# A graph-attention kernel: scores and exponential of a unit set a round ahead of its weights and sums

## The chip, the cores and the metric

The kernel runs on one core of a Trainium2 chip. A core has five engines with an instruction stream each: TensorE (PE, with its weight loads shown as PEld), VectorE (DVE), ScalarE (ACT), GpSimd (POOL) and SyncE (SP); sixteen DMA engines move data for the queues of SP, ACT and POOL. Each engine takes its instructions in order and waits on semaphores of the others. The metric is the device time of one execution in microseconds (us), lower is better; the time stated is the median of three runs.

## The reference

Three layers of graph attention with one head over N = 6250 nodes of D = 64 features and 206250 edges that come ordered by target node (`dst`); between the layers a normalisation, and at the end the logarithm of a softmax, the residual and a last normalisation:

```
def _transformer_conv(x, src, dst, edge_attr, Wq, bq, Wk, bk, Wv, bv, We, Ws, bs):
    q = x @ Wq + bq
    k = x @ Wk + bk
    v = x @ Wv + bv
    e = edge_attr @ We
    kj = k[src] + e
    alpha = jnp.sum(q[dst] * kj, axis=-1) / jnp.sqrt(jnp.float32(D))
    amax = jax.ops.segment_max(alpha, dst, num_segments=N)
    p = jnp.exp(alpha - amax[dst])
    denom = jax.ops.segment_sum(p, dst, num_segments=N)
    w = p / denom[dst]
    msg = (v[src] + e) * w[:, None]
    agg = jax.ops.segment_sum(msg, dst, num_segments=N)
    return agg + x @ Ws + bs

for i in range(L):
    x = _transformer_conv(x, src, dst, edge_attr, Wq[i], ...)
    x = jax.nn.relu(x)
    if i < L - 1:
        x = _layer_norm(x, ln_gamma[i], ln_beta[i])
return jax.nn.log_softmax(x, axis=1)
```

## The kernel before

The edges are cut into chunks of 512, four chunks (`LB`) to a *unit*. A loop goes over the units of a layer, one unit a *round*; the order of instructions on every engine is the order in which the program writes them (a manual schedule), so the calls in the loop of `main_path` are the order of the work.

For one unit, with features of the source nodes beside edge features in a buffer `feat` (edges on partitions):

- `turn(0)` and `turn(1)`: TensorE transposes two chunks each into a PSUM tile of tag "a" (L1517), ScalarE copies them into `featT` (L1520); the edge half of `featT` comes by a load of SP from `eaS` (`across`, L1496).
- `scores`: four matmuls mark in which of a chunk's 32 node slots each edge lies (L1528), four more multiply the queries `q` with `featT` (L1530), into the PSUM tile `ps_s`. The four chunks use the four groups of 32 columns of the array. VectorE takes the maximum `most` (L1537) and its negative (L1539), ScalarE the exponential `prob` (L1541). `prob` has one buffer.
- `weights`: TensorE transposes `prob` (L1549); the copy `probT` (L1552) is ScalarE's in layer 0 and VectorE's in layers 1 and 2. `probT` has one buffer.
- `sums`: sixteen matmuls of `probT` with `feat` (L1562), copied by ScalarE to `part` (L1570). A later `store` writes it to tables in DRAM (L1576). After its sums a unit's `feat` is free: `room` starts the load of the edge half of a later unit into that buffer (`fetch`, SP, L558). There are four buffers (`FB`).

In round u the turns are those of unit u, while scores, weights and sums are those of unit u-1, in this order: turn 0, scores, a bank of picks, turn 1, weights, naturals, a second bank, sums. So weights wait in the same round for the scores' maximum and exponential.

Beside this run, in every round:

- Gathers. GpSimd fetches rows of source nodes by indirect DMA (L609), each released by a small ScalarE copy, the *gate* (L608), which `drip` and `free` place between other work. Layer 0 gathers twelve times a unit, two units ahead.
- Picks and naturals. For part of the edges the source rows come from SBUF: VectorE writes one-hot masks `hot` (six for a bank, L1208, `aim`), TensorE multiplies them with the node table (twelve matmuls, L1234, `bank`), ScalarE copies the result to `kept` (L1241). In odd rounds `naturals` turns `kept` into features of the next pair of units (L1251), which VectorE copies into `feat` (L1268, L1270).
- In layer 0 alone: sorting. `move` advances a generator that sorts the edge features of a later unit with bf16 matmuls against masks `hit` that VectorE makes (`hit` L992, products L1004, stamps L1013, twice a round one half), drains them by ScalarE (`to` L1024, `eT` L1027 and their DMA issues L1028 and L1031), transposes and writes them (L1037, L1039, L1042), and computes indices (L1050, L1052, `src_b` L1053).

Between layers the last three units run in a tail, node features are finished and written (`finish`), and the first loads of the next layer start. PSUM has a tile ring for each tag ("a", "g", "m", "p", "s", "x").

Of the kernel before, what the change touches and what calls it, by code (L numbers as in the profile page):

```python
# [9 lines left out]
F32 = mybir.dt.float32  # L10
# [9 lines left out]
P = 128  # L20
D = 64
L = 3
# [406 lines left out]
def main_path(  # L429
# [123 lines left out]
    def fetch(layer, k):  # L553

        c0, m = batches[k]
        feat = feats.tile([P, LB * T * 2 * D], F32, name="feat")
        if placed(layer, k):
            nc.sync.dma_start(feat[:, LB * T * D :], eaP[k])  # L558
        if layer or placed(layer, k):
            feat = feat.rearrange("p (h c t d) -> p c t h d", h=2, c=LB, d=D)  # L560
        else:
            feat = feat.rearrange("p (c t h d) -> p c t h d", h=2, c=LB, d=D)
        if not placed(layer, k):
            nc.sync.dma_start(
                feat[:, :m, :, 1].rearrange("p c t d -> p (c t) d"),
                ea[c0 : c0 + m].rearrange("c (t p) d -> p (c t) d", p=P),
            )
        loaded[layer, k] = feat
# [604 lines left out]
    class Picker:  # L1173
# [25 lines left out]
        def aim(self):  # L1199

            self.load()
            if not self.aims or self.aims[0][:2] not in self.keys or self.hots:
                return
            k, t, i = self.aims.pop(0)
            made = []
            for h in range(BW):
                hot = picks.tile([P, 2 * PAIR * W], F32R, name="hot", bufs=BW)
                nc.vector.tensor_scalar(  # L1208
                    hot,
                    self.keys[k, t][:, 2 * i * PAIR * W : 2 * (i + 1) * PAIR * W],  # L1210
                    rank[:, h : h + 1],
                    None,
                    ALU.is_equal,
                )
                made.append(hot)
            self.hots[k, t, i] = made
            if i == QUARTERS // 2 - 1:
                del self.keys[k, t]
            self.load()

        def bank(self, tag="x"):

            if not self.banks:
                return
            self.aim()
            k, t, i = self.banks.pop(0)
            made = self.hots.pop((k, t, i))
            px = ps(tag)
            for q in range(2):
                for h in range(BW):  # L1230
                    b = (t * QUARTERS + 2 * i + q) * BW + h
                    assert halved[b] == self.layer
                    cols = slice(q * PAIR * W, (q + 1) * PAIR * W)
                    nc.tensor.matmul(  # L1234
                        px[:, cols],
                        halves[b >= EARLY][:, b - EARLY * (b >= EARLY)].rearrange("p h d -> p (h d)"),
                        made[h][:, cols],
                        start=(h == 0),
                        stop=(h == BW - 1),
                    )  # L1240
            nc.scalar.copy(  # L1241
                kept[t][:, :, 2 * i : 2 * i + 2].rearrange("p c q e -> p q c e"),
                px.rearrange("p (q c e) -> p q c e", q=2, e=W),
            )
            if self.layer:
                self.aim()

        def natural(self, k, t, c, out):

# [199 lines left out]
    class Unit:  # L1449
# [73 lines left out]
        def scores(self, bank):  # L1523
            n = self.rows
            self.p_s = ps(bank)
            quarters = [slice(slot(j) * W, (slot(j) + 1) * W) for j in range(n // W)]
            for j, rows in enumerate(quarters):
                nc.tensor.matmul(self.p_s[rows], codeT[:, rows], self.to, start=True, stop=(j >= self.m))  # L1528
            for j, rows in enumerate(quarters[: self.m]):
                nc.tensor.matmul(  # L1530
                    self.p_s[rows], self.q[:, j * STRIDE : j * STRIDE + W], self.featT[:, j, :], start=False, stop=True
                )
# [4 lines left out]
            nc.vector.tensor_reduce(top[:n], self.p_s[:n], AX.X, ALU.max)  # L1537
            neg = self.part[:n, P : P + 1]
            nc.vector.tensor_scalar(neg, top[:n], -1.0, -M_INIT, ALU.mult, ALU.min)  # L1539
            self.prob = work.tile([P, CH], F32, name="prob", bufs=1)  # L1540
            nc.scalar.activation(  # L1541
                self.prob[:n], self.p_s[:n], AF.Exp, bias=neg, accum_out=self.part[:n, P + 1 : P + 2]
            )

        def weights(self):
# [70 lines left out]
    def serve():  # L1616

        while rooms:
            layer, k = rooms[0]
            if k < len(batches):  # L1620
# [1 line left out]
                    return  # L1622
                fetch(layer, k)
                await_turn(layer, k)
            elif layer + 1 < L and k - len(batches) < FB:
                if not layer and k - len(batches) not in moved:
                    return
                fetch(layer + 1, k - len(batches))
# [13 lines left out]
    class Line:  # L1642
# [7 lines left out]
        def sums(self, to):  # L1650
            for u in range(self.summed, to):
                chunks[self.layer, u].sums()
                if units[u][1] == LB or u == NU - 1:
                    room(self.layer, u + FB if units[u][1] == LB else len(batches) - 1 + FB)
                self.summed = u + 1

        def weights(self, to):
# [1 line left out]
                chunks[self.layer, u].weights()  # L1659
                self.weighed = u + 1  # L1660

        def scores(self, to, bank="s"):
            for u in range(self.scored, to):
                chunks[self.layer, u].scores(bank)
                self.scored = u + 1

        def store(self):
# [19 lines left out]
    for layer in range(L):  # L1687
# [13 lines left out]
        for u in range(NU - 3):  # L1701
# [4 lines left out]
            line.store()  # L1706
            if waiting:
                active.append(waiting.pop(0))
            close_up()
            points = [0]  # L1710
            this.turn(0, lambda: drip(u))
            close_up(3) if close else step()
            move(paces[0])
            if not layer:
                drip(u, 2)
            move(paces[1])
            line.scores(u)
# [21 lines left out]
            move(paces[3])  # L1739
            if not layer:  # L1740
                drip(u, 2)
            line.sums(u)
            free(u, LB - 1)
            picker.aim()

        more = layer + 1 < L
        for _ in sorting:
# [126 lines left out]
```

## Time and profile before

| | us |
|---|---|
| median of three runs | 5328.32 |
| lowest and highest of them | 5322.16, 5331.89 |
| the profiled execution | 5337.1 |
| its span on the core | 5335.4 |
| first round of layer 0 to its last | 119 to 2453 |
| the same in layer 1 | 2524 to 3881 |
| the same in layer 2 | 3955 to 5291 |

The mean granted clock of TensorE in the profiled execution was 0.857 of full speed. The profile's groups give for a line, engine and operation the number of instructions, their busy time and mean length, and then the idle time of that engine just before them with what ended most of it ("<-ACT prob L1541": the engine was idle until ScalarE's instruction of line 1541 that writes `prob`). "issue" stands for idle time in which the engine waited for nothing that the profile shows; "remote" for a semaphore event whose origin is not among the core's recorded instructions. Ends of matmuls are modelled. An fp32 matmul shows as two records. The recorded chain of waits is empty for this execution, so the argument goes by groups, stretches and timelines.

### The profile page before, as it was taken

To read this page: it belongs to the slowest core of one execution; us is meant where nothing else is said; L and a number is where in the kernel's file an instruction comes from. 1 tells how busy PE (TensorE), PEld (TensorE's weight loads), DVE (VectorE), ACT (ScalarE), POOL (GpSimd) and SP (SyncE) were. 2 spreads that over 40 slices of the span, in tenths; PEclk is the share of its full clock that TensorE was granted. 3 is DMA by queue.
4 is the path that set the end of the run, shared out by engine and by line. 5 is a ranking of instruction groups with operands and counts; after the bars stand their busy time and mean duration, and the time that the engine had idled before them with its cause. 6 is when DMAs were issued, how large, how long until landed. Compare 5 with 4: busy or idle time off the path is not lost.

```text
span 5335.4 us, 105267 instructions
## 1 busy us (share of the span) xinstructions
PE 4095.7 (77%) x33967; PEld 2681.4 (50%) x33967; DVE 3172.4 (59%) x8763; ACT 2099.4 (39%) x6475; POOL 2914.4 (55%) x2863
## 2 busy tenths in 40 slices
PE   5677777777777777776788888888768878887876
PEld 3344444444444444444565555555545555555553
DVE  5556666566666656554566656666445666666664
ACT  1233344334434334333344444444333444444443
POOL 4445555555555545553666566665536666666663
PEclk9788999889999988887888888888878888888887
DMA  6555665566666556553555555555435555555553
GB/s 138 138 142 138 157 159 149 151 156 157 156 155 160 149 154 159 141 154 99 126 138 137 127 135 138 140 137 128 120 89 134 135 131 136 137 139 135 135 136 85
DMA packets 749708, 737.55 MB, mean 138 GB/s; under 512 B 390960, under 2 KB 501578, under 8 KB 749150
## 3 DMA queue, kind: packets, MB, share of 16 engines
q1 hardware_dynamic: 565854, 510.70, 38.3%
q0 software_dynamic: 91264, 93.64, 10.3%
q10 hardware_dynamic: 92032, 126.38, 7.1%
q8 instruction: 276, 4.52, 0.4%
q14 instruction: 282, 2.31, 0.1%
HBM read 570.27 MB, written 160.07 MB: 137 GB/s over the span
## 4 chain that ended last, share of the span: by engine, by line


## 5 line engine op out<-in xcount | busy, mean ns | idle before, releaser
L609 POOL DMA_INDIRECT feat<-x,gate x1608 | 1661.9, 1033 | 1055.6 <-ACT gate L608 556.5
L609 POOL DMA_INDIRECT feat<-in_x,gate x1212 | 1218.1, 1005 | 1199.3 <-ACT gate L608 534.3
L1208 DVE TENSOR_SCALAR hot<-key,rank 128x512 fp32r<-128x512 f16 x2976 | 1254.1, 487 | 284.6 <-remote 104.7
L1234 PE MATMUL ps_x<-hot,halves 128*128 128x256 f32 x4800 | 845.3, 322 | 35.9 <-issue 17.8
L1234 PEld LDWEIGHTS ps_x<-hot,halves 128*128 128x128 f32 x4800 | 704.3, 214 | 321.8 <-issue 178.1
L1520 ACT COPY featT<-ps_a 64x512 f32<-64x512 f32 x1192 | 690.4, 579 | 172.5 <-issue 47.3
L1537 DVE TENSOR_REDUCE most<-ps_s 128x1 f32<-128x512 f32 x297 | 205.0, 690 | 813.1 <-PE ps_s L1530 447.6
L1562 PE MATMUL ps_g<-feat,probT 128*32 128x128 f32 x9672 | 512.3, 309 | 212.6 <-issue 161.1
L1530 PE MATMUL ps_s<-featT,q 128*32 128x512 f32 x2376 | 517.3, 727 | 57.6 <-issue 49.5
L608 ACT COPY gate<-src_b 128x1 int32<-128x1 int32 x2772 | 501.8, 191 | 122.4 <-issue 52.2
L1241 ACT CAST kept<-ps_x 128x512 fp32r<-128x512 f32 x400 | 234.8, 587 | 792.1 <-remote 511.9
L1004 PE MATMUL ps_x<-hit,rest 128*64 128x512 bf16 x3200 | 534.2, 414 | 4.0 <-issue 3.7
L1562 PEld LDWEIGHTS ps_g<-feat,probT 128*32 128x32 f32 x9672 | 337.2, 122 | 360.4 <-issue 253.1
L1541 ACT ACTIVATE prob<-ps_s,part 128x512 f32<-128x512 f32 x297 | 204.4, 688 | 760.6 <-DVE part L1539 520.2
L1549 PE MATMUL ps_p<-ident,prob 128*128 128x128 f32 (+1 forms) x1224 | 218.8, 306 | 347.1 <-ACT prob L1541 283.3
L992 DVE TENSOR_SCALAR hit<-ruler,pos 128x512 bf16<-128x512 f16 x1600 | 483.1, 373 | 2.7 <-remote 2.7
L1517 PE MATMUL ps_a<-ident,feat 128*128 128x128 f32 x2380 | 438.1, 307 | 45.0 <-issue 30.9
L1517 PEld LDWEIGHTS ps_a<-ident,feat 128*128 128x128 f32 x2380 | 303.8, 157 | 171.3 <-issue 128.2
L1004 PE MATMUL ps_x<-hit,raw 128*64 128x512 bf16 x1600 | 347.4, 427 | 8.6 <-issue 8.6
L1549 PEld LDWEIGHTS ps_p<-ident,prob 128*128 128x128 f32 (+1 forms) x1224 | 144.3, 152 | 402.5 <-ACT prob L1541 322.6
L1004 PEld LDWEIGHTS <-rest 128*64 128x64 bf16 x3200 | 201.2, 121 | 181.2 <-issue 59.0
L1570 ACT COPY part<-ps_g 128x128 f32<-128x128 f32 (+1 forms) x309 | 81.4, 263 | 408.2 <-remote 115.0
(235 smaller groups left out, 4618.5 us busy)
## 6 DMA issues: line engine op xcount, KB each, us to landing
feat<-eaP SPq DMA_DIRECT2D x296, 512.0 KB
featT<-eaS SPq DMA_DIRECT2D x296, 512.0 KB
key<-keyS SPq DMA_DIRECT2D x248, 256.0 KB
raw<-in_ea SPq DMA_DIRECT2D x200, 256.0 KB
eaS<-eT ACTq DMA_DIRECT2D x200, 256.0 KB
eaP<-eN ACTq DMA_DIRECT2D x200, 256.0 KB
feat<-x,gate POOLq DMA_INDIRECT x1608
part<-part SPq DMA_DIRECT2D x600, 32.5 KB
```

What stands on the lines that cost most here:

```text
L608: copy(gate, index[:, i + t : i + t + 1])
L609: nc.gpsimd.indirect_dma_start(out=loaded[layer, k][:, c, t, 0], out_offset=None, in_=xts[layer][:, :], in_offset=bass.IndirectOffsetOnAxi ...
L992: nc.vector.tensor_scalar(hit, ruler, self.pos[:, at : at + 1], None, ALU.is_equal)
L1004: nc.tensor.matmul(self.px[i][j * D : (j + 1) * D, :], self.part(i, part)[:, (j * T + t) * D : (j * T + t + 1) * D], self.hits[t, 2 * i + ...
L1208: nc.vector.tensor_scalar(hot, self.keys[k, t][:, 2 * i * PAIR * W : 2 * (i + 1) * PAIR * W], rank[:, h : h + 1], None, ALU.is_equal,)
L1234: nc.tensor.matmul(px[:, cols], halves[b >= EARLY][:, b - EARLY * (b >= EARLY)].rearrange("p h d -> p (h d)"), made[h][:, cols], start=(h ...
L1241: nc.scalar.copy(kept[t][:, :, 2 * i : 2 * i + 2].rearrange("p c q e -> p q c e"), px.rearrange("p (q c e) -> p q c e", q=2, e=W),)
L1517: nc.tensor.transpose(pt[:, j - js[0], t // 2], rows[:, t * D : (t + 2) * D], ident)
L1520: nc.scalar.copy(featT[:, :, :, h, :], pt[h * D : (h + 1) * D])
L1530: nc.tensor.matmul(self.p_s[rows], self.q[:, j * STRIDE : j * STRIDE + W], self.featT[:, j, :], start=False, stop=True)
L1549: nc.tensor.transpose(p_t[:, t, :n], self.prob[:n, t * P : (t + 1) * P], ident[:n, :n])
L1562: nc.tensor.matmul(p_g[rows, :].rearrange("n (h d) -> n h d", h=2), self.probT[:, t, rows], batch[:, c + j, t], start=(t == 0), stop=(t == ...
```

## The change

In round u the weights (transposes and copy) and the sums are now those of unit u-2, while the scores remain those of unit u-1. Weights open the round, the sums stand before the scores, and the exponential is a method of its own, `exps`, called after turn 1. The new order in a round: weights (u-2), turn 0, in layers 1 and 2 a bank, sums (u-2), scores (u-1), in layer 0's odd rounds a bank, turn 1, exponential (u-1), naturals, a bank.

With it: naturals and the second bank use the PSUM tag "p" in place of "s"; in layers 1 and 2 the masks of a bank may be made two banks ahead, with a second set of six `hot` buffers in the pool `later`; a fifth feature buffer in layers 1 and 2, also in `later` (every fifth batch uses it), so that `room` and `serve` count five there; the gates of layer 0 stand at other places of the round (`drip`); at a layer switch one more batch is fetched. In the tail weights precede sums. Lines from about 557 on move by 3 to 10.

```
-        feat = feats.tile([P, LB * T * 2 * D], F32, name="feat")
+        more = layer and ((layer - 1) * len(batches) + k) % (FB + 1) == FB
+        feat = later.tile([P, LB * T * 2 * D], F32, name="feat") if more else feats.tile(
+            [P, LB * T * 2 * D], F32, name="feat"
+        )
...
-            if not self.aims or self.aims[0][:2] not in self.keys or self.hots:
+            if not self.aims or self.aims[0][:2] not in self.keys or len(self.hots) > (self.layer > 0):
...
+            pool = later if self.layer and i % 2 else picks
...
-                hot = picks.tile([P, 2 * PAIR * W], F32R, name="hot", bufs=BW)
+                hot = pool.tile([P, 2 * PAIR * W], F32R, name="hot", bufs=BW)
...
-            self.aim()
+            if self.banks[0] not in self.hots:
+                self.aim()
...
-            if self.layer:
-                self.aim()
...
+        def exps(self):
+            n = self.rows
             self.prob = work.tile([P, CH], F32, name="prob", bufs=1)
             nc.scalar.activation(
...
-            elif layer + 1 < L and k - len(batches) < FB:
+            elif layer + 1 < L and k - len(batches) < FB + (layer > 0):
...
-                    room(self.layer, u + FB if units[u][1] == LB else len(batches) - 1 + FB)
+                    held = FB + (self.layer > 0)
+                    room(self.layer, u + held if units[u][1] == LB else len(batches) - 1 + held)
...
+            line.weights(u - 1)
+            if layer:
+                picker.aim()
+            points = [0]
             close_up()
-            points = [0]
             this.turn(0, lambda: drip(u))
             close_up(3) if close else step()
             move(paces[0])
-            if not layer:
-                drip(u, 2)
-            move(paces[1])
-            line.scores(u)
-            drip(u)
             if layer:
                 picker.bank()
-            elif odd:
+                picker.aim()
+            drip(u, 1 if layer else 2)
+            line.sums(u - 1)
+            drip(u)
+            move(paces[1])
+            line.scores(u, exps=False)
+            if not layer and odd:
                 picker.bank("g")
-            drip(u)
+            if not layer:
+                drip(u)
             ask(layer, u + 1)
             chunks[layer, u + 1].across()
             close_up() if close else step()
             this.turn(1, lambda: drip(u))
-            line.weights(u)
+            if u:
+                chunks[layer, u - 1].exps()
+            drip(u)
             close_up(3) if close else step()
             move(paces[2])
+            if not layer:
+                drip(u)
             if odd:
-                picker.naturals(u + 1, "ms" if layer else "s")
+                picker.naturals(u + 1, "mp" if layer else "p")
             if layer:
                 picker.bank()
             elif not odd and u + 2 >= U0:
-                picker.bank("s")
-            drip(u)
+                picker.bank("p")
             picker.load()
             move(paces[3])
-            if not layer:
-                drip(u, 2)
-            line.sums(u)
             free(u, LB - 1)
-            picker.aim()
+            if not layer:
+                picker.aim()
...
         u = NU - 3
+        line.weights(u - 1)
         line.sums(u - 1)
-        line.weights(u - 1)
         line.scores(u)
...
-            for k in range(FB):
+            for k in range(FB + 1):
```

More of the change, by code (lines that the diff above doesn't have):

```diff
@@ L1539, in scores @@
             nc.vector.tensor_scalar(neg, top[:n], -1.0, -M_INIT, ALU.mult, ALU.min)
+        def exps(self):
+            n = self.rows
             self.prob = work.tile([P, CH], F32, name="prob", bufs=1)
             nc.scalar.activation(
-                self.prob[:n], self.p_s[:n], AF.Exp, bias=neg, accum_out=self.part[:n, P + 1 : P + 2]
+                self.prob[:n],
+                self.p_s[:n],
+                AF.Exp,
+                bias=self.part[:n, P : P + 1],
+                accum_out=self.part[:n, P + 1 : P + 2],
             )
@@ L1660, in weights, with scores @@
                 self.weighed = u + 1
-        def scores(self, to, bank="s"):
+        def scores(self, to, bank="s", exps=True):
             for u in range(self.scored, to):
                 chunks[self.layer, u].scores(bank)
+                if exps:
+                    chunks[self.layer, u].exps()
                 self.scored = u + 1
@@ L1735, in main_path @@
             elif not odd and u + 2 >= U0:
-                picker.bank("s")
-            drip(u)
+                picker.bank("p")
             picker.load()
             move(paces[3])
+            free(u, LB - 1)
             if not layer:
-                drip(u, 2)
-            line.sums(u)
-            free(u, LB - 1)
-            picker.aim()
+                picker.aim()
         more = layer + 1 < L
```

## The prediction

> **What bounds the kernel now.** I read the page first, then the stretches by stage, then the groups of each layer, and last the timeline of two rounds. The page gives the profiled execution's own span and TensorE's load:
>
> ```profile
> span 5335.4 us, 105267 instructions
> ...
> PE 4095.7 (77%) x33967; PEld 2681.4 (50%) x33967; DVE 3172.4 (59%) x8763; ACT 2099.4 (39%) x6475; POOL 2914.4 (55%) x2863
> ```
>
> TensorE is the busiest, at 77%. The stretches from the first to the last full round of each layer (columns: stretch, its length, busy time and count of PE, PEld, DVE, ACT, POOL, granted clock, DMA share, GB/s):
>
> ```profile
> 119.00:2453.00 2334.00, 1759.14 (x15331) 1048.19 (x15329) 1414.67 (x4317) 901.70 (x2741) 1181.26 (x1174) 0.88 0.59 151
> ...
> 2524.00:3881.00 1357.00, 1097.61 (x8878) 764.41 (x8874) 796.11 (x1925) 540.48 (x1736) 822.77 (x796) 0.84 0.55 132
> ...
> 3955.00:5291.00 1336.00, 1061.49 (x8720) 754.25 (x8716) 796.03 (x1962) 565.27 (x1768) 820.25 (x796) 0.84 0.56 132
> ```
>
> With 98 rounds a layer (392 transposes of `prob` below, four a round) a round takes 23.8, 13.8 and 13.6 us. Matmuls divided by length give 15331/2334 = 6.57, 8878/1357 = 6.54 and 8720/1336 = 6.53 per us. Three stages, one of them with quite other work, go at one matmul rate within 0.6%. That may be chance, or a limit on how fast TensorE is fed; it matters because the change leaves TensorE's matmuls as many as they were. Now the waits of TensorE that the change is about, for layers 0, 1 and 2 in turn:
>
> ```profile
> L1549 PEld LDWEIGHTS ps_p<-ident,prob 128*128 128x128 f32 x392 | 52.4, 169 | 206.9 <-ACT prob L1541 195.8 <-issue 10.7
> ```
> ```profile
> L1562 PEld LDWEIGHTS ps_g<-feat,probT 128*32 128x32 f32 x3136 | 112.9, 126 | 139.8 <-issue 105.1 <-DVE probT L1552 21.8 <-DVE hot L1208 2.4
> ...
> L1549 PEld LDWEIGHTS ps_p<-ident,prob 128*128 128x128 f32 x392 | 42.2, 142 | 68.8 <-ACT prob L1541 45.4 <-issue 16.5 <-ACT gate L608 3.1
> ```
> ```profile
> L1562 PEld LDWEIGHTS ps_g<-feat,probT 128*32 128x32 f32 x3136 | 114.8, 130 | 147.3 <-issue 106.2 <-DVE probT L1552 28.2 <-DVE hot L1208 2.7
> ...
> L1549 PEld LDWEIGHTS ps_p<-ident,prob 128*128 128x128 f32 x392 | 43.9, 145 | 105.4 <-ACT prob L1541 60.8 <-issue 40.5 <-ACT gate L608 2.6
> ```
>
> The wait for the exponential is 195.8 + 45.4 + 60.8 = 302 us, that for the copied weights 21.8 + 28.2 = 50 us. What is in it shows in two neighbouring rounds of layer 0 (start, length, engine, line, operation, in brackets the idle time before):
>
> ```profile
> 1214.40 0.40 PE L1528 MATMUL ps_s<-to,codeT 128*32 128x512 bf16 x4
> ...
> 1214.62 1.04 PE L1530 MATMUL ps_s<-featT,q 128*32 128x512 f32 x8
> ...
> 1215.60 0.66 PE L1517 MATMUL ps_a<-ident,feat 128*128 128x128 f32 x4
> ...
> 1221.76 0.69 DVE L1537 TENSOR_REDUCE most<-ps_s 128x1 f32<-128x512 f32 x1 [7.31 <-remote]
> ...
> 1223.57 0.71 PEld L1549 LDWEIGHTS ps_p<-ident,prob 128*128 128x128 f32 x4 [7.55 <-ACT prob L1541]
> ...
> 1223.99 1.27 DVE L992 TENSOR_SCALAR hit<-ruler,pos 128x512 bf16<-128x512 f16 x4
> ```
> ```profile
> 1235.34 0.41 PE L1004 MATMUL ps_x<-hit,raw 128*64 128x512 bf16 x2
> ...
> 1238.06 0.61 PE L1013 MATMUL ps_m<-hit,stamp 128*32 128x512 bf16 x8
> ...
> 1238.50 0.87 PE L1528 MATMUL ps_s<-to,codeT 128*32 128x512 bf16 x3
> ...
> 1243.97 1.07 PE L1530 MATMUL ps_s<-featT,q 128*32 128x512 f32 x4 [0.37 <-issue]
> ...
> 1244.96 1.70 PE L1234 MATMUL ps_g<-hot,halves 128*128 128x256 f32 x12
> 1245.07 0.69 DVE L1537 TENSOR_REDUCE most<-ps_s 128x1 f32<-128x512 f32 x1 [6.23 <-PE ps_s L1530]
> ```
>
> In the first the scores seem done at 1214.62 + 1.04 = 1215.66, yet the maximum, which waits for nothing else, starts at 1221.76. In the second the same matmuls come out one by one until 1245. From first score matmul to maximum it is 7.36 us the one way and 6.57 the other. So about 6 us of lateness sits in the score matmuls and no dependence in the program explains it; only 1223.57 - 1221.76 = 1.81 us of the "wait for prob" of 7.55 us is the chain of maximum and exponential. Two longer stretches of layer 0 agree (lines first of 600 to 830 us, then of 1980 to 2210):
>
> ```profile
> L1549 PEld LDWEIGHTS ps_p<-ident,prob 128*128 128x128 f32 x42 | 5.2, 159 | 19.7 <-ACT prob L1541 19.6
> L1530 PEld LDWEIGHTS ps_s<-featT,q 128*32 128x32 f32 x80 | 4.7, 118 | 19.7 <-issue 18.5
> ```
> ```profile
> L1549 PEld LDWEIGHTS ps_p<-ident,prob 128*128 128x128 f32 x36 | 5.2, 181 | 31.0 <-ACT prob L1541 28.5 <-issue 2.5
> ...
> L1530 PEld LDWEIGHTS ps_s<-featT,q 128*32 128x32 f32 x72 | 2.7, 110 | 5.8 <-issue 4.2
> ```
> ```profile
> 600.00:830.00 230.00, 176.77 (x1559) 104.04 (x1560) 148.93 (x454) 91.27 (x281) 117.44 (x120) 0.92 0.60 154
> ...
> 1980.00:2210.00 230.00, 173.67 (x1534) 108.92 (x1536) 145.44 (x460) 91.63 (x276) 120.25 (x120) 0.85 0.59 154
> ```
>
> Exponential wait plus slow issue is 19.7 + 19.7 = 39.4 us in one and 31.0 + 5.8 = 36.8 in the other: what the one loses the other gains, and the matmuls done stay 1559 and 1534. This is the strongest line against a large gain.
>
> **The change part by part.**
>
> Transposes and sums a round later (layer 0). What surely goes is the chain of 1.81 us less what already covers it, the 0.66 us of the second turn's transposes, in the even rounds (in odd ones the twelve picks stand there as well): 49 x 1.15 = 56 us. Bounds: 0 (all comes back as slow issue) and 196 (the whole wait goes). I take 56, since the two stretches show the rest to be lateness of the scores.
>
> A new wait: the sums now stand soon after the sorting matmuls, and the copy `probT`, on ScalarE in this layer, stands behind the copies `to` and `eT`, the issues of their transfers and two gates:
>
> ```profile
> L1027 ACT COPY eT<-ps_x 128x512 f32<-128x512 f32 x196 | 106.0, 598 | 0.0
> ...
> L1552 ACT COPY probT<-ps_p 128x512 f32<-128x512 f32 x98 | 57.5, 587 | 6.8 <-PE ps_s L1234 3.0 <-PE ps_a L1037 0.8 <-remote 0.8
> L1024 ACT CAST to<-ps_m 128x512 bf16<-128x512 f32 x98 | 57.4, 586 | 353.7 <-PE ps_m L1013 249.9 <-remote 103.4 <-issue 0.4
> ```
> ```profile
> 1232.46 0.89 ACTq L1031 DMA_DIRECT2D eaS<-eT  x2
> 1232.51 0.60 PE L1517 MATMUL ps_a<-ident,feat 128*128 128x128 f32 x4
> ...
> 1233.73 0.19 ACT L608 COPY gate<-src_b 128x1 int32<-128x1 int32 x1
> ...
> 1234.46 0.27 PE L1050 MATMUL ps_a<-to,keyc 128*4 128x256 bf16 x1 [1.36 <-ACT wT L1379]
> ...
> 1234.78 0.64 PE L1037 MATMUL ps_m<-ident,eT 128*128 128x128 f32 x4
> ```
>
> ScalarE needs 0.59 + 2 x 0.60 + 0.89 + 2 x 0.19 + 0.59 = 3.6 us; TensorE has 0.71 + 0.60 + 0.27 + 0.64 = 2.2 us of other work there, and the 0.27 needs `to` itself. So the wait is between 0 and 1.4 us a round; I take 0.4, near the lower end, because the index matmul waited already (1.36 us in this row): +39 us, bounds 0 and 137. Behind the waiting sums stand the scores, and behind them VectorE's maximum.
>
> Layers 1 and 2. Here both waits lose their cause: prob is made most of a round ahead, and `probT` has the first turn and twelve picks before its sums. Together 106 + 50 = 156 us. The best stretch of these layers caps it:
>
> ```profile
> 3440.00:3580.00 140.00, 117.95 (x968) 80.43 (x966) 85.73 (x209) 58.08 (x190) 88.58 (x85) 0.89 0.58 139
> ```
>
> 968/140 = 6.91 matmuls per us; all 17598 at that rate take 2545 us instead of 2693, so -148. The lower end is what the copy alone gives, -50. Between them I take the middle, -99. Neither POOL nor VectorE stands in the way: 822.8/98 = 8.4 us of gathers and 796/98 = 8.1 us of VectorE in rounds of 13.6.
>
> Buffers, picks, gates, loads. The fifth feature buffer and the second set of `hot` buffers add no instruction but one earlier load at each of two layer switches, which lies beside the 70 us of the switch: 0. Layer 0 keeps four buffers while its sums come half a round later, so the gates of POOL come in a burst behind them. POOL has 1181/98 = 12.1 us of gathers in a round of 23.8, so a burst from mid-round on runs a little into the next round, while the unit it serves is turned a round later: 0; it would cost only what exceeded that round. On SyncE the fetch behind the sums now waits in mid-round, ahead of the next unit's loads of `to`, `q` and `featT`, which are needed a round on: 0. If that cover went, the next scores would be late by it.
>
> Sum: 5337.1 - 56 + 39 - 99 = 5221 against its own 5337.1 us (span 5335.4). That execution lies 0.16% above the median of 5328.3, so I forecast 5212.
>
> A rule speaks to the feed of TensorE. The Trainium skill, "TensorE: Matmul & The Clock Gate", section "Wait — 56ns, not 53.3ns?", says that without hardware decode the sequencer spends about 62 ns on each MATMUL, which bounds short ones. By it 33967 matmuls would need an estimated 2106 us, which would bound nothing here and leave the sum as it is; the trace shows one matmul every 152 ns, so it neither confirms nor needs that rule.
>
> **The rivals.**
>
> *The whole wait goes.* If the late scores are themselves hidden once nobody on TensorE waits for them, 302 + 50 us go less 39: 5337 - 313 = 5024, or 5016 by the median. For it: the engine whose work is named in the wait is freed of it. Against: the two stretches above.
>
> *TensorE's feed is the bound.* Then every stall removed returns as slow issue and the change doesn't do what it says: 5320. For it: the three equal rates. Against: 6.91 in one stretch and 6.57 on the mean.
>
> *VectorE becomes late in layer 0 (slower).* The sums and transposes now stand ahead of the scores, so the maximum comes later against the sorting, and VectorE, in order, has the `hit` masks of the next products behind it.
>
> ```profile
> L992 DVE TENSOR_SCALAR hit<-ruler,pos 128x512 bf16<-128x512 f16 x1600 | 483.1, 373 | 2.7 <-remote 2.7
> ```
>
> Eight masks are 8 x 0.373 = 3.0 us and begin 1223.99 - 1221.76 = 2.2 us after the maximum does; with the maximum 6.1 us late they are done 11.3 us after the scores. TensorE reaches the products that need them after one half of the products (1238.06 - 1235.34 = 2.7 us), their stamps (0.6), a turn (0.7), picks (1.7), transposes (0.7), the other turn (0.6), index and rows (0.9) and the sums (125.4/98 = 1.3):
>
> ```profile
> L1562 PE MATMUL ps_g<-feat,probT 128*32 128x128 f32 x3136 | 125.4, 276 | 24.5 <-issue 24.3
> ```
>
> That is 9.2 us, so up to 2.1 us of waiting a round, 206 us in 98. Added to the sum it gives up to 5427, or 5418 by the median; with three quarters of it 5376, or 5367. It decides from 116/98 = 1.2 us a round on. For it: the lateness seen at 1221.76. Against: VectorE itself was late for nobody in the rows above, and not every score comes late.
>
> **How the numbers follow.** The forecast's case (5100 to 5300) has 0.40, the whole wait 0.25, the feed 0.14, VectorE 0.21. A measurement here can tell 0.2%, some 11 us, from no change. Of the feed's case about half lies within it and half below, and of VectorE's 0.02 within: faster 0.40 + 0.25 + 0.06 = 0.71, same 0.09, slower 0.20. For 8 in 10 the range reaches from 4970, which leaves out what lies below the whole wait's figure by more than 1%, to 5380, which takes in three quarters of VectorE's wait. The forecast's own range is 5100 to 5300.
>
> **What would show it.** The row of L1549's successor should name prob no more (below 20 us of 302), in all layers; if the time still stands, "issue" at score and sum matmuls must have grown by as much. The matmul rate of layers 1 and 2 should be 6.7 to 6.9, of layer 0 6.6. The sums' weight loads in layer 0 should wait for `probT` by some 39 us. If VectorE's rival holds, the products' loads wait for `hit` by over 100 us. I am wrong if layer 0 shortens by more than 100 us, or if a wait not named here takes more than 50.

## The result, and the profile after

The changed kernel takes 5406.59 us (median of 4 runs, 5394.08 to 5430.11) against 5325.24 us for the one before (4 runs): ratio 1.0149, 95% interval 1.0126 to 1.0173. It is 1.5% slower, where 2.2% faster was forecast. The profiled execution has a span of 5404.6 us against 5335.4.

```profile
span 5404.6 us, 103984 instructions
...
PE 3985.8 (74%) x33967; PEld 2727.0 (50%) x33967; DVE 3126.5 (58%) x8763; ACT 2111.1 (39%) x6475; POOL 3037.5 (56%) x2863
```

TensorE's matmuls are as many as before. Where the 69 us of span lie shows in the stretches from the first to the last score maximum of each layer's loop, first of before, then of after (length, then busy time and count of PE, PEld, DVE, ACT, POOL, clock, DMA share, GB/s):

```profile
118.90:2432.80 2313.90, 1747.49 (x15231) 1042.22 (x15229) 1410.78 (x4306) 894.77 (x2722) 1175.58 (x1168) 0.88 0.59 151
2524.50:3855.40 1330.90, 1085.07 (x8819) 760.93 (x8820) 792.05 (x1915) 536.92 (x1721) 810.44 (x784) 0.84 0.55 132
3955.50:5273.00 1317.50, 1050.69 (x8665) 750.68 (x8666) 794.47 (x1960) 562.43 (x1755) 808.64 (x783) 0.85 0.56 133
```
```profile
111.30:2419.20 2307.90, 1769.55 (x15243) 1040.97 (x15241) 1397.91 (x4305) 893.42 (x2724) 1210.45 (x1164) 0.84 0.59 151
2523.20:3874.80 1351.60, 1012.04 (x8802) 780.51 (x8802) 771.91 (x1903) 543.73 (x1721) 844.28 (x784) 0.85 0.55 130
3972.20:5349.60 1377.40, 1002.28 (x8656) 772.42 (x8656) 772.86 (x1948) 567.64 (x1755) 844.62 (x788) 0.83 0.54 127
```

Layer 0 is 6 us shorter, layer 1 is 21 and layer 2 is 60 us longer, the rest 5 shorter. The waits behind it, weight loads by group, first of layer 0 before (L1251 are the naturals):

```profile
L1004 PEld LDWEIGHTS <-rest 128*64 128x64 bf16 x3120 | 194.0, 120 | 175.3 <-issue 55.2 <-DVE hit L992 1.5 <-DVE spare L934 1.0
...
L1004 PEld LDWEIGHTS <-raw 128*64 128x64 bf16 x1560 | 96.0, 119 | 103.7 <-issue 46.0 <-DMA part<-part 0.8 <-DMA part<-empty 0.6
...
L1251 PEld LDWEIGHTS ps_s<-twice,kept 128*128 128x128 f32 x384 | 54.8, 205 | 33.7 <-DVE feat L1270 23.4 <-issue 10.4
L1549 PEld LDWEIGHTS ps_p<-ident,prob 128*128 128x128 f32 x388 | 51.7, 168 | 196.8 <-ACT prob L1541 185.7 <-issue 10.7
...
L1530 PEld LDWEIGHTS ps_s<-featT,q 128*32 128x32 f32 x776 | 38.1, 111 | 133.3 <-issue 118.3
```

then of layer 0 after, where L1007 are the products (L1004 before), L1533 the scores (L1530), L1559 the transposes of prob (L1549), L1572 the sums (L1562) and L1254 the naturals (L1251):

```profile
L1007 PEld LDWEIGHTS <-rest 128*64 128x64 bf16 x3120 | 214.5, 127 | 259.1 <-issue 168.1 <-DVE spare L944 1.2 <-DVE ge L878 0.7
...
L1559 PEld LDWEIGHTS ps_p<-ident,prob 128*128 128x128 f32 x388 | 45.1, 151 | 91.1 <-issue 45.9 <-ACT kept L1246 39.9 <-ACT gate L611 5.2
...
L1533 PEld LDWEIGHTS ps_s<-featT,q 128*32 128x32 f32 x776 | 23.4, 110 | 19.7 <-issue 0.2
```
```profile
L1007 PEld LDWEIGHTS <-raw 128*64 128x64 bf16 x1560 | 107.4, 125 | 153.7 <-issue 99.4 <-DMA eaS<-eT 2.5 <-DMA keyS<-key 1.9
L1572 PEld LDWEIGHTS ps_g<-feat,probT 128*32 128x32 f32 x3104 | 106.8, 138 | 59.7 <-ACT probT L1562 25.0 <-ACT gate L611 14.4 <-issue 13.0
...
L1254 PEld LDWEIGHTS ps_p<-twice,kept 128*128 128x128 f32 x384 | 70.5, 257 | 90.6 <-DVE feat L1273 48.9 <-ACT kept L1246 26.2 <-issue 14.1
```

In layer 0 the 185.7 us of waiting for prob are gone, and the slow issue of the scores too (118.3 to 0.2). Idle time by "issue" at the products has grown instead, from 55.2 + 46.0 = 101 to 168.1 + 99.4 = 268 us, and some came back as dependences: transposes and naturals now wait 39.9 + 26.2 = 66 us for ScalarE's copy `kept`, and the naturals' wait for VectorE's `feat` has doubled (23.4 to 48.9). The round stays as long as it was. The granted clock of this stretch was lower as well, 0.84 against 0.88; what that cost is not separated. Layers 1 and 2 after:

```profile
L1559 PEld LDWEIGHTS ps_p<-ident,prob 128*128 128x128 f32 x388 | 52.3, 167 | 169.3 <-ACT prob L1547 87.4 <-issue 57.9 <-ACT kept L1246 13.5
```
```profile
L1559 PEld LDWEIGHTS ps_p<-ident,prob 128*128 128x128 f32 x388 | 51.6, 166 | 193.3 <-ACT prob L1547 107.0 <-issue 51.5 <-ACT gate L611 31.6
```

The wait for prob, to be removed, has grown there from 45.4 + 60.8 = 106 (the prediction's rows, over slightly longer stretches) to 87.4 + 107.0 = 194 us. ScalarE's own groups in layer 1 show a part of why: ahead of the exponential now stand the copies of turn 1, and these wait for TensorE's transposes. Before, then after:

```profile
L1520 ACT COPY featT<-ps_a 64x512 f32<-64x512 f32 x388 | 225.2, 580 | 78.2 <-issue 36.3 <-PE ps_x L1234 13.3 <-ACT gate L608 6.5
```
```profile
L1523 ACT COPY featT<-ps_a 64x512 f32<-64x512 f32 x388 | 225.6, 582 | 207.4 <-PE ps_a L1520 111.7 <-remote 42.2 <-PE ps_x L1239 25.2
```

The exponential itself hardly waits any more (19.5 us in layer 1 against 98.3): its wait has moved into the copies ahead of it, and the weights that need its result now open the next round.

### The profile page after: what moved, and what is told of

It is laid out like the page before. It is cut to its first block, busy times and chain, and to the rows that moved or that the text cites. A ratio compares the mean times of both kernels' runs of the same rounds, so it can differ in the third digit from the quotient of the medians.

```text
span 5404.6 us, 103984 instructions
## 1 busy us (share of the span) xinstructions
PE 3985.8 (74%) x33967; PEld 2727.0 (50%) x33967; DVE 3126.5 (58%) x8763; ACT 2111.1 (39%) x6475; POOL 3037.5 (56%) x2863
## 4 chain that ended last, share of the span: by engine, by line
## 5 line engine op out<-in xcount | busy, mean ns | idle before, releaser
L612 POOL DMA_INDIRECT feat<-x,gate x1608 | 1731.6, 1077 | 1057.0 <-ACT gate L611 532.6
L612 POOL DMA_INDIRECT feat<-in_x,gate x1212 | 1257.1, 1037 | 1148.0 <-ACT gate L611 855.0
L1239 PE MATMUL ps_x<-hot,halves 128*128 128x256 f32 x4800 | 783.1, 319 | 6.5 <-issue 4.9
L1572 PE MATMUL ps_g<-feat,probT 128*32 128x128 f32 x9672 | 509.7, 318 | 355.8 <-issue 200.4
L1007 PE MATMUL ps_x<-hit,rest 128*64 128x512 bf16 x3200 | 594.1, 440 | 45.4 <-issue 43.8
L1572 PEld LDWEIGHTS ps_g<-feat,probT 128*32 128x32 f32 x9672 | 336.2, 126 | 478.4 <-issue 273.2
L1559 PE MATMUL ps_p<-ident,prob 128*128 128x128 f32 (+1 forms) x1224 | 237.6, 324 | 390.4 <-ACT prob L1547 187.2
L611 ACT COPY gate<-src_b 128x1 int32<-128x1 int32 x2772 | 473.6, 191 | 84.1 <-ACT eT L1030 44.6
L1562 DVE COPY probT<-ps_p 128x512 f32<-128x512 f32 x204 | 140.3, 688 | 566.6 <-issue 153.5
L1533 PE MATMUL ps_s<-featT,q 128*32 128x512 f32 x2376 | 438.5, 700 | 12.0 <-issue 9.4
L1007 PE MATMUL ps_x<-hit,raw 128*64 128x512 bf16 x1600 | 384.9, 453 | 32.7 <-issue 25.6
L1559 PEld LDWEIGHTS ps_p<-ident,prob 128*128 128x128 f32 (+1 forms) x1224 | 156.0, 161 | 470.3 <-ACT prob L1547 207.6
L1007 PEld LDWEIGHTS <-rest 128*64 128x64 bf16 x3200 | 221.2, 127 | 264.3 <-issue 171.1
L1254 PE MATMUL ps_p<-twice,kept 128*128 128x64 f32 x1168 | 199.6, 312 | 83.1 <-DVE feat L1273 44.8
```

What stands on the lines that cost most here:

```text
L611: copy(gate, index[:, i + t : i + t + 1])
L612: nc.gpsimd.indirect_dma_start(out=loaded[layer, k][:, c, t, 0], out_offset=None, in_=xts[layer][:, :], in_offset=bass.IndirectOffsetOnAxi ...
L1007: nc.tensor.matmul(self.px[i][j * D : (j + 1) * D, :], self.part(i, part)[:, (j * T + t) * D : (j * T + t + 1) * D], self.hits[t, 2 * i + ...
L1239: nc.tensor.matmul(px[:, cols], halves[b >= EARLY][:, b - EARLY * (b >= EARLY)].rearrange("p h d -> p (h d)"), made[h][:, cols], start=(h ...
L1533: nc.tensor.matmul(self.p_s[rows], self.q[:, j * STRIDE : j * STRIDE + W], self.featT[:, j, :], start=False, stop=True)
L1559: nc.tensor.transpose(p_t[:, t, :n], self.prob[:n, t * P : (t + 1) * P], ident[:n, :n])
```

## The experiments

One plain fact must be known to read them. The experiments ran on five chips (the record doesn't name the one of the first measurement), and on each of them the kernel before took 4336 to 4347 us, not 5325. "These chips" below means those five. Every ratio below is against the kernel before on the same chip.

**More instructions for TensorE.** Theory: TensorE's instructions come at a limited mean rate, which would explain the three equal rates. Rival: array work and dependences.

```
+            for i in range(4):
+                for rows in quarters:
+                    nc.tensor.matmul(self.p_s[rows, :W], codeT[:, rows], self.to[:, :W], start=True, stop=True)
             for j, rows in enumerate(quarters):
                 nc.tensor.matmul(self.p_s[rows], codeT[:, rows], self.to, start=True, stop=(j >= self.m))
```

> The kernel before, with 16 more tiny matmuls (32 columns, overwritten by the real ones) ahead of every unit's score matmuls: 306 x 16 = 4896 more weight loads and matmuls, with almost no array work. Feed theory (TensorE takes its instructions at a limited mean rate, one load and matmul per 152 ns of span): 4896 x 0.152 = +744 us. Array and dependence theory: the four 4-column matmuls of the index take 0.25 us, so 16 cost about 1 us a unit where TensorE is on the path: between 0 and +300 us.

Measured: 4352.35 us, ratio 1.0027 (1.0006 to 1.0048). A second time on another chip:

> The kernel before with 4896 tiny loads and matmuls more, a second time, to meet the condition of the first measurement if it comes up. If before takes about 5325 us in this job: +744 us by the feed theory, 0 to +300 by the other. If before takes about 4340: +0.0 to +0.5% as on the first chip it ran on, and the condition of 5325 stays untried.

4349.37 us, ratio 0.9998 (0.9975 to 1.0020). With four full-width matmuls in place of sixteen tiny ones:

> The kernel before, with 4 more matmuls of full width (512 columns) ahead of every unit's score matmuls, a copy of the four that mark the slots: 1224 more loads and matmuls, a quarter of the other kernel's instructions, with more array work. Feed theory: 1224 x 0.152 = +186 us, a quarter of the other. Array theory: 0.40 us a unit by the four's own row (0.85 if one after the other), 0 to +260 us, and not less than the other kernel.

4362.62 us, ratio 1.0044 (1.0017 to 1.0070). Nearly 5000 loads and matmuls more cost at most 0.5%, some 21 us where the feed theory says 744, and the second run shows no cost at all; the four wide ones cost 7 to 30 us. No limit on the number of instructions is met on these chips. Why TensorE went at 6.55 matmuls per us in the first measurement is not answered by this, since that condition did not come up again.

**The profile of before on these chips.** 

> The kernel before once more, for its profile beside the other runs. Chip theory: where 'before' takes about 4342 us, the slow single issue of score and sum matmuls (intervals of 0.70 us) is all but gone from its trace and TensorE goes at over 8.0 matmuls per us, where the recorded one went at 6.55. GpSimd theory for layers 1 and 2 there: 8 gathers of 1.04 us with 0.30 us between them are 10.7 us, and the round is within 0.5 us of it.

4348.37 us. Stretches of the three loops, then one round's scores:

```profile
99.90:1973.90 1874.00, 1519.89 (x15225) 933.39 (x15224) 1411.55 (x4306) 891.60 (x2722) 1194.95 (x1163) 0.93 0.73 186
2062.50:3133.80 1071.30, 931.86 (x8819) 734.71 (x8820) 785.29 (x1916) 540.00 (x1721) 830.09 (x782) 0.88 0.68 165
3222.30:4296.00 1073.70, 903.81 (x8665) 715.89 (x8666) 789.28 (x1959) 565.65 (x1755) 831.86 (x785) 0.88 0.68 163
```
```profile
1013.90 1.03 PE L1530 MATMUL ps_s<-featT,q 128*32 128x512 f32 x8
...
1015.01 0.69 DVE L1537 TENSOR_REDUCE most<-ps_s 128x1 f32<-128x512 f32 x1 [1.27 <-PE ps_s L1530]
```

TensorE does 15225/1874 = 8.12 matmuls per us. The scores end at 1014.93 and the maximum starts 0.08 us later, not 6.10. The lateness that the forecast found in the score matmuls isn't in this round, and the scores' slow issue in layer 0, 118.3 us there, is 3.0 us in this profile. It came with the first measurement's condition, not with the kernel alone. GpSimd's waits in layer 1 (total, times, longest) and its gathers:

```profile
POOL feat L609 <- issue: 119.8, 393, 0.3
POOL feat L609 <- ACT gate L608: 57.5, 179, 3.2
```
```profile
L609 POOL DMA_INDIRECT feat<-x,gate x782 | 830.7, 1062 | 241.3 <-issue 119.5 <-ACT gate L608 57.5 <-DMA feat<-x,gate 31.1
```

Busy and idle time together, 830.7 + 241.3 = 1072.0 us, must fill the stretch of 1071.3 us; what tells is how the idle time is spread. It is 0.31 us ahead of each of the 782 gathers. Counted over the trace, one gather of this layer waits longer than 0.4 us, against 195 in layer 1 of the first measurement. So GpSimd goes from gather to gather without a rest: here it is the bound of layers 1 and 2, and in the first measurement it can't be the only one.

**The changed kernel on these chips, and each half of it.**

> The changed kernel on this chip. Feed theory (the limit on TensorE's issue took the gain): without that limit the dependence sum applies, 150 to 313 us below before. GpSimd theory: layers 1 and 2 are bound by the gathers, only layer 0 can gain, 0.3 us in 98 rounds: within 1% of before, on either side. If this chip is the slower one: 5406 against 5325.

> The changed kernel with the order of before in layer 0 alone. If layers 1 and 2 carry the loss (16 and 60 us of it by the stage times), this is as slow as the changed kernel or slower: +1.0 to +2.0% against before. If layer 0 carries it, it is within 0.3% of before.

> The changed kernel with the order, masks and four buffers of before in layers 1 and 2, the new order in layer 0. If layers 1 and 2 carry the loss: within 0.3% of before, or below it by what layer 0 gains, up to 1%. If layer 0 carries it: +1 to +2%.

The round's body stands twice, the new one under the condition and that of before under `else`; shown is the new order in layer 0 only, and its opposite has `if layer:`. The kernel with the new order in layer 0 only also has the masks and the four buffers of before, so its layers 1 and 2 are those of before but for the tail.

```
+            if not layer:
...
+            else:
...
```

| kernel | us | ratio (95% interval) |
|---|---|---|
| changed | 4359.45 | 1.0045 (1.0030 to 1.0060) |
| new order in layers 1 and 2 only | 4412.74 | 1.0162 (1.0127 to 1.0196) |
| new order in layer 0 only, masks and buffers of before | 4289.75 | 0.9878 (0.9858 to 0.9898) |

The two halves have opposite signs: the change in layer 0 gains 1.2%, the change in layers 1 and 2, order, masks and buffers together, loses 1.6%. The last kernel beats the one before and the changed one. The changed kernel's loops and its gathers in layer 1:

```profile
101.00:1936.50 1835.50, 1540.07 (x15229) 935.14 (x15229) 1402.76 (x4306) 889.34 (x2723) 1214.91 (x1163) 0.92 0.74 190
2033.40:3129.20 1095.80, 866.68 (x8807) 706.38 (x8806) 768.85 (x1905) 548.58 (x1724) 856.99 (x784) 0.90 0.68 161
3223.90:4302.90 1079.00, 858.40 (x8653) 714.14 (x8654) 769.05 (x1947) 568.47 (x1756) 841.46 (x780) 0.88 0.69 162
```
```profile
L612 POOL DMA_INDIRECT feat<-x,gate x784 | 857.0, 1093 | 238.9 <-issue 111.2 <-ACT gate L611 49.7 <-DMA feat<-x,gate 36.9
```

Layer 0 is 38.5 us shorter. Layer 1 is 24.5 us longer, and its gathers are busy 857.0 - 830.7 = 26.3 us longer, for a mean of 1093 ns against 1062: the loss of this layer is in the gathers themselves. Layer 2 is 5 us longer, and the two switches between the layers, from last maximum to first, are 14.5 us longer together. A stretch of the changed kernel's timeline, VectorE's masks and GpSimd alone:

```profile
2857.43 0.94 POOL L612 DMA_INDIRECT feat<-x,gate  x1 [0.30 <-issue]
...
2857.52 2.68 DVE L1212 TENSOR_SCALAR hot<-key,rank 128x512 fp32r<-128x512 f16 x6
...
2858.68 1.25 POOL L612 DMA_INDIRECT feat<-x,gate  x1 [0.30 <-ACT gate L611]
...
2860.23 3.06 POOL L612 DMA_INDIRECT feat<-x,gate  x1 [0.31 <-ACT gate L611]
...
2860.72 2.44 DVE L1212 TENSOR_SCALAR hot<-key,rank 128x512 fp32r<-128x512 f16 x6
...
2863.60 0.94 POOL L612 DMA_INDIRECT feat<-x,gate  x1 [0.30 <-issue]
...
2869.31 4.83 DVE L1212 TENSOR_SCALAR hot<-key,rank 128x512 fp32r<-128x512 f16 x12
```

A gather beside no mask, as at 2863.60, takes 0.94 us. One beside masks mostly takes 1.25, though not always: that at 2857.43 took 0.94 with a run of masks beginning 0.09 us after it. Counted over layer 1 of this trace, 99% of the gathers beside no mask stay below 1.0 us, and 15% of those that run beside masks throughout, whose median is 1.25. One gather that meets the second of two runs close together took 3.06 us: it ended at 2863.29, just after the run at 2863.16. The change sets both aims of a round close together, so such runs and even one of twelve occur. Of all gathers of layers 1 and 2, 28 of 1563 took over 2 us in the changed kernel, and 17 of these end 0.12 us after a run of masks. In the kernel before 10 of 1566 did, all 2.32 us long and none ending so, hence held by something else that isn't known. In layer 1 these long gathers exceed 0.945 us each by 31.9 us in all, against 8.3 in the kernel before: they make nearly all of the 26.3 us.

**The masks apart.** 

```
                 picker.bank()
-                picker.aim()
...
                 chunks[layer, u - 1].exps()
+            if layer:
+                picker.aim()
```

> The changed kernel, where in layers 1 and 2 the second set of six masks is made after turn 1 instead of right behind the first bank, so that twelve masks no longer stand in one run on VectorE. Contention theory (gathers are 0.95 us beside no mask and 1.23 us beside masks in the changed kernel, 1.14 in the one before): the mean gather falls from 1.10 us to 1.07 or less and layers 1 and 2 to 11.0 us a round, so 40 to 60 us below the changed kernel on a chip where GpSimd is the bound; the time is then at or below before (0.985 to 1.000). Rival, the loss is the order of weights and sums: no change, 1.004 or more.

> The changed kernel with the two sets of masks apart, a second time, on whatever chip this job gets. If before takes about 4340 us: 0.985 to 0.995 again. If before takes about 5325 us: feed theory 0.995 to 1.005, for the gathers bind nothing there; if the runs of twelve masks cost there too, 0.985 to 0.995.

4294.61 us, ratio 0.9905 (0.9873 to 0.9937), and again 4306.96, 0.9906 (0.9885 to 0.9928). Loops and gathers of layer 1 of the first:

```profile
99.50:1914.00 1814.50, 1532.59 (x15227) 931.03 (x15226) 1403.30 (x4305) 890.50 (x2723) 1221.06 (x1163) 0.92 0.74 192
2010.60:3078.00 1067.40, 866.23 (x8807) 708.43 (x8807) 765.76 (x1910) 547.63 (x1724) 828.31 (x785) 0.91 0.66 165
3170.90:4232.60 1061.70, 846.16 (x8654) 701.22 (x8654) 771.10 (x1954) 569.29 (x1756) 824.32 (x779) 0.90 0.66 164
```
```profile
L612 POOL DMA_INDIRECT feat<-x,gate x785 | 828.9, 1056 | 239.2 <-issue 117.0 <-ACT gate L611 48.8 <-DMA feat<-x,gate 40.5
```

One call moved: the mean gather falls to 1056 ns, layer 1 to 1067.4 us and layer 2 to 1061.7, both a little below before, and 7 gathers of 1563 exceed 2 us, none of them ending with a run of masks. With the pair on one chip below under "Four buffers", this shows the contention of gathers with runs of masks close together as the cause of the loss in these layers on these chips; with the masks apart the order of weights and sums costs nothing there. It gains nothing that is sure either: 0.9905 here, 0.9878 with layers 1 and 2 as before, on another chip.

**The exponential early.**

```
-            line.scores(u, exps=False)
+            line.scores(u)
...
-            if u:
-                chunks[layer, u - 1].exps()
```

> The changed kernel with the exponential back right behind the scores' maximum, ahead of the second turn's copies on ScalarE; weights and sums stay a round later. If the exponential's place behind those copies is what makes layers 1 and 2 longer (waits for prob of 87 and 107 us there), these waits go and the time falls by 60 to 150 us against the changed kernel, to 5330 or below. If TensorE's feed is the bound, the waits for prob go and come back as issue, and the time stays between 5330 and 5410.

4378.73 us, ratio 1.0085 (1.0059 to 1.0111). The wait for prob in layer 1 falls to 59.9 us from 85.0 in the changed kernel on its chip, and layer 1 stays at 1096 us. So its place behind the copies makes a part of the wait, 25 us, what makes the rest isn't shown, and it is not what costs these layers here. Whether it is in the first condition, where the wait is about as long (87.4 us) but GpSimd not the bound, was not tried.

**Longer GpSimd work.**

```
+            if layer:
+                nc.gpsimd.memset(pad, 0.0)
...
+    pad = const.tile([P, 16], F32, name="pad")
```

> The kernel before, with one tiny fill of 16 elements a partition on GpSimd behind each gather of layers 1 and 2 (1608 of them). GpSimd theory: each adds its own length and the pause, some 0.1 to 0.2 us, to the path, +150 to +320 us on a chip where GpSimd is without idle time in these layers. Rival, something else paces these layers: below +50 us. On the chip of the first measurement, where GpSimd waits for gates a quarter of the time, below +50 us by both.

4366.66 us, ratio 1.0063 (1.0041 to 1.0086): 31 us, far from the expected 150, and by the bounds set beforehand on the side of the rival, that something else paces these layers. What follows is a reading after the fact. The fill took the place of most of the pause:

```profile
L609 POOL DMA_INDIRECT feat<-x,gate x782 | 834.1, 1067 | 100.4 <-issue 67.1 <-ACT gate L608 18.4 <-PE ps_x L1237 5.6
L616 POOL MEMSET pad<- 128x16 f32 x782 | 160.8, 206 | 0.3
```

The idle time ahead of a gather falls from 0.31 to 0.13 us, and the 0.21 us of the fill stand there instead; a few fills overlap a gather in the records. Layer 1 grew by 16 us (1087.3 against 1071.3). That agrees with GpSimd as the bound, but it is a small push and doesn't prove it; the unbroken row of gathers and the masks apart say it better.

**Less array work in layer 0.** Two of three products go over 32 columns; the rest of the remainders is left out.

```
-                                self.px[i][j * D : (j + 1) * D, :],
+                                self.px[i][j * D : (j + 1) * D, :wide],
...
-                                self.hits[t, 2 * i + j],
+                                self.hits[t, 2 * i + j][:, :wide],
...
```

> The kernel before, where in the sorting of layer 0 two of three products go over 32 columns in place of 512 (the two small remainders of the edge features are left out for the other columns): as many instructions, a good part of the array work gone. A half's 24 products take 2.7 us at best; two thirds of them in two halves of 98 rounds are about 350 us of TensorE's time. Feed theory: within 1% of before. Array theory: down by 150 to 350 us.

4288.83 us, ratio 0.9882 (0.9835 to 0.9929), layer 0 62 us shorter (1811.8 against 1874.0). The feed theory's bound of 1% is just missed (the interval reaches 0.9929), the array theory's 150 us clearly: TensorE's busy time there falls by 183 us (1336.76 against 1519.89) and a third of that reaches the end, at a lower granted clock (0.85 in this stretch against 0.93). TensorE's array is one of several things on the path in layer 0.

**Four buffers.**

```
-        more = layer and ((layer - 1) * len(batches) + k) % (FB + 1) == FB
+        more = False
...
-            for k in range(FB + 1):
+            for k in range(FB):
...
```

> The changed kernel with four feature buffers in all layers and no fifth load at a layer switch. If the fifth buffer's earlier load is what lengthens the two switches (63 us each against 56 and 58 before): switches back to 56 to 58, 5 to 13 us less than the changed kernel. If the fifth buffer feeds the gathers (GpSimd has no idle time with it): without it GpSimd waits for gates again and layers 1 and 2 grow by 20 us or more.

> The same four buffers, with the two sets of masks apart (the second set behind turn 1). Contention theory: layers 1 and 2 as in the kernel with the masks apart (1067 and 1062 us), mean gather 1.06 us, 0.985 to 0.993 of before. If the fifth buffer is needed for that: layers 1 and 2 longer by 20 us or more.

4338.41 us, ratio 1.0000 (0.9983 to 1.0017), and with the masks apart 4307.56, 0.9902 (0.9863 to 0.9940). These two ran on one chip and differ by the place of the one call alone. Layer 1 and its gathers, masks close together, then apart:

```profile
2019.60:3114.40 1094.80, 874.17 (x8807) 713.18 (x8806) 769.35 (x1905) 549.87 (x1724) 852.53 (x783) 0.89 0.66 161
```
```profile
L612 POOL DMA_INDIRECT feat<-x,gate x783 | 853.2, 1090 | 242.4 <-issue 118.5 <-ACT gate L611 42.2 <-DMA feat<-x,gate 31.1
```
```profile
2039.80:3112.20 1072.40, 860.46 (x8808) 700.39 (x8809) 765.46 (x1910) 547.45 (x1724) 830.05 (x783) 0.92 0.67 164
```
```profile
L612 POOL DMA_INDIRECT feat<-x,gate x783 | 831.0, 1061 | 242.4 <-issue 118.0 <-ACT gate L611 43.0 <-DMA feat<-x,gate 42.1
```

The layer is 22.4 us shorter and its gathers are busy 22.2 us less. The fifth buffer is not needed: with the masks apart, layers 1 and 2 take 1072.4 and 1061.8 us without it. With four buffers and the masks close together the switches between the layers, from last maximum to first, stay long (95.6 and 94.9 us, where before has 88.6 and 88.5), so the fifth buffer's early load is not what lengthens them; that cause stays open. With all masks close together the buffer even seems to cost some 0.4%, but that is a comparison over two chips.

## Why the prediction was wrong

*Layer 0, -56 and +39.* The direction of the sum was right and its size of no matter: -6 us in the first condition. The +39 was of the right size: the sums wait 25.0 us for `probT`. The forecast said that the wait's larger part is lateness that would come back as issue. Much of it did: for 186 us of prob and 118 of slow issue at the scores, 166 us of issue at the products and some 90 us of new waits for `kept` and `feat`. There the rival "TensorE's feed is the bound" came nearest for this layer, in that the removed stalls returned; that a limit on instructions is the mechanism isn't shown. On the other chips the layer gains 38.5 us, where the two terms give 17.

*Layers 1 and 2, -99: the step that failed.* "Here both waits lose their cause" is false: both waits grew, 106 to 194 us for prob and, in the groups of the sums, 21.8 + 28.2 = 50 to 28.3 + 44.1 = 72 us for the copied weights. The step counted most of a round between exponential and transposes; in fact the exponential stands behind turn 1's copies on ScalarE, which takes its instructions in order, and its reader opens the very next round. (With the exponential ahead of those copies about 60 of 85 us of the wait remained in layer 1, so they are not the whole of it.) On the five chips it was as wrong, though GpSimd sets the time there: in the rows of prob's transposes the wait for it grew from 30.8 + 50.1 = 81 to 85.0 + 100.2 = 185 us. In the first measurement these layers became 81 us longer. How much of the 81 is that wait and how much are longer gathers (1077 ns against 1033 on the page) it leaves open. The held gathers are there too: 51 of 1570 took over 2 us, against 4 of 1566, and GpSimd was busy 70 us longer. But GpSimd waited for gates as well (252 us in layer 1), and TensorE waited for a gather's landing only 11 us in both layers, as little as before.

*"Neither POOL nor VectorE stands in the way."* This was the same step's second mistake. It divided the gathers' busy time by the rounds (8.4 us) and left out the 0.30 us ahead of each and what the moved masks would add. On the five chips a round's eight gathers with their pauses are 11.0 us, which is the whole round, and the change makes them longer. In the first measurement a round had 13.6 us, so there this is not shown to be what failed.

*The buffers, 0.* The fifth buffer was right at nothing for its load; a second set of masks was not: by the program it is what lets both aims stand close together. The switches, taken at nothing, grew by 14.5 us on one of the five chips, from a cause that stays open.

*VectorE late in layer 0.* This rival, the only one on the slower side, named the wrong place: the products' weight loads wait for `hit` below 3 us in all, where it needed over 100. That the time came out on its side was luck. The rival that the whole wait goes, -313, came true in no run.

## What to carry to other kernels

Where two engines work side by side, ask of a moved instruction not only who waits for it but what it now runs beside: two runs of six masks close together held single gathers of another engine up to 2.5 us longer. Set an engine's busy time together with the pauses between its instructions against the round before calling it free. Before working out a gain from waits, see whether the waits are the kernel's own: the largest one here, for prob in layer 0, was half as long on the five chips (92.9 us against 185.7).

## What the runs showed of the hardware

The same kernel took 5325 us in one measurement and 4336 to 4347 us on five chips. VectorE, ScalarE and lone gathers are as long in both (maximum 0.69 us, gather 0.94 us). The difference of the two profiles, 989 us, is at TensorE: its matmuls are busy 546 us longer (4095.7 against 3549.4) and idle by "issue" 461 us, against nothing, with score matmuls in some rounds coming out singly or their results reaching VectorE 6 us late. The mean granted clock was 0.857 against 0.897. What causes it isn't known.

A gather on GpSimd takes 0.94 us alone and mostly about 1.25 us beside VectorE's masks (f16 in, 512 columns out). Where two runs of masks stand close together or twelve in one, it may be held until a run ends (3.06 us in the row above, 3.46 at most in those two layers). Between the layers of the kernel with the masks apart, a run of eighteen masks of 7.21 us held one for 6.69 us. It has a pause of 0.30 us ahead of it, most of which a small fill of 0.21 us on the same engine can use.
